# One token group of the shared expert moved behind the routed experts

## The chip, the cores and the metric

The kernel runs on one core of a Trainium2 chip. The core has a matrix engine (TensorE, PE in the profile), a vector engine (VectorE, DVE), an activation engine (ScalarE, ACT), a general one (GpSimd, POOL) and a synchronising one that here only issues transfers (SyncE, SP). Each runs its own stream of instructions in order and waits for the others on semaphores. Weights, tokens and results lie in device memory (HBM); work is done in on-chip memory (SBUF) and in the accumulators of TensorE (PSUM). The metric is the device time of the kernel in microseconds.

## The reference

Inputs are `x`, 32 sequences of 100 tokens of 512 values, and a context of which the causal mask leaves the first 100 positions. A layer norm, a cross-attention of 16 heads with an output product `Wfc` and a residual come first. Then, with `hs` the layer norm of that sum:

```
logits = hs @ gate_w.T                      # 16 experts
scores = softmax(logits)                    # per token
topk_w, topk_idx = top_k(scores per sequence and expert, 12)
g, u   = x_tok @ Wg[e].T, x_tok @ Wu[e].T   # the 12 tokens of each sequence, hidden size 1024
eo     = ((gelu(g) * u) @ Wd[e].T) * topk_w
out    = scatter_add(eo)                    # to the tokens they came from
shared = (gelu(hs @ Ws_g.T) * (hs @ Ws_u.T)) @ Ws_d.T
result = x + out + shared
```

Each of the 16 experts so works on 32 x 12 = 384 tokens, three tiles of 128. The shared expert works on all 3200 tokens, 25 tiles.

## The kernel before, in words

All products are in float32, made of three products of split operands (a high part and the remainder): `mm3`, line 55. So every weight and every activation is split once, by a cast on ScalarE and a subtraction on VectorE.

The attention stage (to about 430 us) writes its result to device memory, tensor `yD`. The feed-forward stage is the class `FeedForward`, method `run`. Its order is written out by hand for TensorE, ScalarE, VectorE and SyncE; GpSimd's order is chosen by the scheduler. The stage is a row of jobs: first nine jobs for the shared expert, one for each group of tiles in `GROUPS` (3, 2, 2, 3, 3, 3, 3, 3, 3 tiles), then 16 jobs for the routed experts, each of three tiles.

A job (`job`) has eight steps, one for each 128 hidden values. A step does the gate and up products (`gate_up`, 24 products into the PSUM tiles "gu"), then what is listed for this step under `mid`, then the down products of the step before (`down`, into "dn", 3 products for each tile), then what is listed under `post`. Gelu, multiplication and split (`hidden`: tiles g, hh, hl) run on ScalarE and VectorE while TensorE does the next products. After the last step's down products each tile goes to a sink. A job's last down products stand in step 0 of the next job.

- `shared_sink` adds the product to the residual on VectorE (line 759) and stores the sum to `out` by SyncE (line 760).
- `expert_sink` scales on ScalarE (line 792) and adds into `out` by an indirect transfer that GpSimd issues (line 793).

The lists `mid` and `post` hold the work that goes on beside the products:

- Preparation of the next group (class `Prep`): load y (step 0), load x, add the bias on GpSimd, split y (step 1), the output product `fc` (steps 2 to 4), layer norm `ln` one tile per step, store of the normed token to `xnD`, transposition and split `turn` two steps after `fc`, then `logits` and `tokens` in step 7. `tokens` puts the logits of the group into the table `LG`.
- Routing (class `Route`), in the last group's job: the softmax over `LG` after the job before it, the transposes of the scores (`turn`, line 938, copies of line 940, stores to `sD`) in steps 0 and 1, the load of the scores by sequence (`load`), the top-8 search twice (`top`) and an exchange through `rD` in step 2, the slot lists `isl` and `wsl` (`slots`) in step 4, the gather of expert 0's tokens by GpSimd (line 768), and their transposes (`gturn`, line 779) in step 7.
- In an expert's job: the gather and the transposes of the next expert's tokens.
- Weights: a chunk is the part of gate, up and down weights for one step, 768 KB. `chunk_load` asks for it (line 615, two raw buffers), `chunk_split` splits it (lines 626 and 627) into one of eight buffers `whl`, one per step. The shared expert's eight chunks are split once and stay for all nine groups. From the last group's job on, each step splits the chunk of the next job.

The small PSUM tiles "m" of `fc`, the transposes and the logits share two buffers. The tiles "big" (y, the scores, gathered tokens) share two, the split tokens xh and xl share two, the tiles x1 six.

Of the kernel before, what the change touches and what calls it, by code (L numbers as in the profile page):

```python
# [7 lines left out]
F32 = mybir.dt.float32  # L8
# [3 lines left out]
ALU = mybir.AluOpType  # L12
# [27 lines left out]
def f32(ap):  # L40
    return ap.bitcast(F32)
# [495 lines left out]
class FeedForward:  # L537
# [4 lines left out]
    def __init__(self, tc, K, top):  # L542
        self.tc, self.K, self.nc = tc, K, tc.nc
        self.starts = [sum(GROUPS[:g]) for g in range(len(GROUPS))]
        self.sw, self.raws, self.asked, self.nxt = {}, {}, 0, 0
        self.pend = None
# [12 lines left out]
        self.LG = wfp.tile([128, T // 128, NE], F32, name="LG")  # L559
        self.stacks = [top.enter_context(ExitStack()) for _ in range(3)]  # L560
# [49 lines left out]

    def chunk_load(self):
        n = self.asked
        if n < NFC * (self.K.ne + 1):
            self.raws[n] = self.rawp.tile([128, 3 * D], F32, name="wraw")
            self.nc.sync.dma_start(self.raws[n], self.K.wE[n // NFC, n % NFC])
            self.asked += 1

    def chunk_split(self, n, part=None):
# [79 lines left out]

    def run(self):
        self.open_rest()  # L700
        ng = len(GROUPS)
        for g, nt in enumerate(GROUPS):
            mid, post = {}, {}

            def at(d, f, *calls):
                d.setdefault(f, []).extend(calls)

            if g == 0:
                for f in range(NFC - 2):
                    at(post, f, lambda f=f: self.chunk_split(f + 2))  # L710
            if g + 1 < ng:
                p = self.prep(g + 1)
                at(post, 0, p.load_y, *[lambda i=i: p.load_x(i) for i in range(p.nt)])
                at(post, 1, *[lambda i=i: p.bias(i) for i in range(p.nt)])
                at(post, 1, p.split_y)
                for i in range(p.nt):
                    at(mid, 2 + i, lambda p=p, i=i: p.fc(i))
                    at(post, 2 + i, lambda p=p, i=i: p.ln(i))
                    at(post, 3 + i, lambda p=p, i=i: p.store(i))
                    at(mid, 4 + i, lambda p=p, i=i: p.turn(i))  # L720
                at(mid, 7, p.logits)
                at(post, 7, p.tokens)
            if g == ng - 1:
                r = Route(self)
# [11 lines left out]
            self.job(0, xh, xl, nt, self.shared_sink(self.starts[g], x1s), mid, post)  # L736
            if g + 1 < ng:
                self.ready[g + 1] = p.done()
            if g + 2 == ng:
                Route.softmax(self)  # L740
        self.route = r
        for e in range(self.K.ne):
            mid, post = {}, {}
            if e + 1 < self.K.ne:
                at(post, 0, lambda: self.gather(e + 1, r))
                for i in range(NST):
                    at(mid, 3 + i, lambda i=i: self.gturn(e + 1, i))
                at(post, 0, lambda: self.chunk_split(NFC * (e + 2) - 1))
                for f in range(1, NFC):
                    at(post, f, lambda f=f: self.chunk_split(NFC * (e + 2) + f - 1))  # L750
            else:
                at(post, 0, lambda: self.chunk_split(NFC * (e + 2) - 1))
# [52 lines left out]
class Prep:  # L805
# [30 lines left out]
    def bias(self, i, eng=None):  # L836
        (eng or self.F.nc.gpsimd).tensor_tensor(self.xb[i], self.xb[i], self.F.bfc, ALU.add)  # L837
# [38 lines left out]
    def store(self, i):  # L876
        self.F.nc.sync.dma_start(self.F.K.xn[self.rows(i), :], self.xn[i])

    def turn(self, i):
        F, nc, cs = self.F, self.F.nc, slice(i * 128, (i + 1) * 128)  # L880
        if self.xh is None:
            self.xh, self.xl = F.xt_tiles()
        tv = self.pt()
        for d in range(NC4):
            nc.tensor.transpose(tv[:, d, :], self.xn[i][:, d * 128:(d + 1) * 128], F.K.ident)
        nc.scalar.copy(self.xh[:, :, cs], tv)
        nc.vector.tensor_tensor(self.xl[:, :, cs], tv, f32(self.xh[:, :, cs]), ALU.subtract)
# [23 lines left out]
        return self.xh, self.xl, [self.xb[i] for i in range(self.nt)]  # L911


class Route:


    def __init__(self, F):
        self.F, self.nc = F, F.nc

    @staticmethod  # L920
    def softmax(F):
# [9 lines left out]
    def turn(self, b0, nb):  # L931
        F, nc = self.F, self.nc
        so = F.bigp.tile([128, NC4, GMAX], F32, name="big").rearrange("p c t -> p (c t)")
        for t0 in range(0, nb, 4):
            nt = min(4, nb - t0)
            tb = F.ps_m.tile([128, D], F32, name="m")
            for i in range(nt):
                nc.tensor.transpose(tb[0:NE, i * 128:(i + 1) * 128], F.LG[:, b0 + t0 + i, :],
                                    F.K.ident)
            nc.vector.tensor_copy(so[0:NE, t0 * 128:(t0 + nt) * 128], tb[0:NE, 0:nt * 128])  # L940
        nc.sync.dma_start(F.K.sD[:, b0 * 128:(b0 + nb) * 128], so[0:NE, 0:nb * 128])

    def load(self):
        F, nc = self.F, self.nc
# [38 lines left out]
@with_exitstack  # L983
def tile_kernel(ctx, tc, x, ctxT, wA, wE, bfc, gwT, ident, mask, base, out):
    nc = tc.nc
    K = Env()
    K.nsb, K.ne = NSB, NE
    K.x, K.ctxT, K.wA, K.wE, K.bfc, K.gwT, K.mask, K.base, K.out = \
        x, ctxT, wA, wE, bfc, gwT, mask, base, out
    dram = ctx.enter_context(tc.tile_pool(name="dram", bufs=1, space=bass.MemoryType.DRAM))  # L990
    K.kD = dram.tile([128, NC4, T], F32, name="kD")
    K.vD = dram.tile([T, D], F32, name="vD")
    K.yD = dram.tile([NC4, 128, T], F32, name="yD")
    K.xn = dram.tile([T, D], F32, name="xnD")
    K.sD = dram.tile([NE, T], F32, name="sD")
# [56 lines left out]
```

## Time and profile before

| | |
|---|---|
| Median of three runs | 1749.06 us (1748.99 to 1749.1) |
| The profiled execution | 1750.64 us |
| Its span, first to last instruction | 1748.8 us |
| Granted clock of TensorE | 0.987 |
| TensorE busy | 1698.7 us, 97% |
| VectorE, ScalarE, GpSimd busy | 885.7, 681.2, 445.0 us |
| Moved by all transfers | 211.13 MB, 121 GB/s on average |
| Idle of TensorE from 846.4 to 911.1 us (last group's job, routing) | 64.70 - 59.97 = 4.73 us |
| Idle of TensorE from 489.6 to 536.8 us (a two-tile group) | 47.20 - 46.17 = 1.03 us |

How to read the lines shown below. A line of the timeline has the start, the duration, engine and source line, operation, "output <- inputs" by the program's names, shapes, a count and, in brackets, how long the engine was idle before it and who ended that. A line of the waits has the waiting engine and line, who was waited for, the total in us, the number of waits and the longest. "PE" is the product, "PEld" its weight load, "SPq" or "POOLq" the instruction queue of an engine. Line 1048 is the end of the program: each engine drains, and the engines exchange semaphores. A line of that list has the count, the shortest, middle and longest duration in ns, and the start of the first and of the last.

### The profile page before, as it was taken

What the parts mean: (1) busy time and instruction counts of PE and PEld (TensorE: products, weight loads), DVE (VectorE), ACT (ScalarE), POOL (GpSimd) and SP (SyncE); (2) the same over time, 40 slices, a digit from 0 to 9 for tenths busy, and PEclk for the clock granted to TensorE, in tenths of its full rate; (3) what the DMA queues carried; (4) which work ended last, traced back from release to release, by engine and by line L of the source; (5) the groups of instructions that cost most, each with busy time, mean ns of one, the idle gap of its engine ahead of it and who ended that gap; (6) DMA issues with size and microseconds to landing.
All of it is one profiled execution on the core that took longest, in us unless ns stands there. A gap on an engine that the chain in (4) does not pass through costs nothing.

```text
span 1748.8 us, 27994 instructions
## 1 busy us (share of the span) xinstructions
PE 1698.7 (97%) x11072; PEld 1559.6 (89%) x11072; DVE 885.7 (51%) x2118; ACT 681.2 (39%) x1086; POOL 445.0 (25%) x399
## 2 busy tenths in 40 slices
PE   7999999989999999999999999999999999999996
PEld 6888888878888999999889999999999999999996
DVE  4877777775333333333454444444444444444431
ACT  4555555543112111211234444444444444444431
POOL 3777777661111011101020111110111111011111
PEclk9999999989999999999999999999999999999998
DMA  7444443534111101102154555554555554555531
GB/s 211 136 137 155 131 131 118 164 109 134 70 63 59 55 31 67 61 19 73 46 185 142 163 141 153 158 158 148 148 159 147 163 153 143 156 162 137 137 88 18
DMA packets 82995, 211.13 MB, mean 121 GB/s; under 512 B 9489, under 2 KB 35842, under 8 KB 82864
## 3 DMA queue, kind: packets, MB, share of 16 engines
q1 hardware_dynamic: 71792, 183.87, 32.2%
q0 software_dynamic: 10784, 25.21, 7.9%
q8 instruction: 87, 1.43, 0.3%
q14 instruction: 44, 0.36, 0.1%
q10 hardware_dynamic: 288, 0.27, 0.0%
HBM read 163.71 MB, written 45.60 MB: 120 GB/s over the span
## 4 chain that ended last, share of the span: by engine, by line
PE 91%; DVE 3%; DMA 2%; POOL 2%; ACT 1%; issue 1%; SPq 0%; POOLq 0%; ACTq 0%; DVEq 0%
PE gu L55 46%; PE dn L55 23%; PE kv L55 10%; PE m L55 3%; PE ms L277 2%; PE sc L236 2%; PE ms L292 1%; POOL p L256 1%; DMA big<-yD 1%; PE m L779 1%; DVE p L247 1%; PE ms L167 1%; DVE xt L161 1%; DMA kD<-kk 1%; PE m L894 1%
## 5 line engine op out<-in xcount | busy, mean ns | idle before, releaser
L55 PE MATMUL gu<-xh,whl 128*128 128x384 f32 (+1 forms) x3200 | 645.0, 333 | 1.3 <-ACT g L654 1.3
L55 PEld LDWEIGHTS gu<-xh,whl 128*128 128x128 f32 x3200 | 559.0, 188 | 18.8 <-ACT g L654 1.5
L55 PE MATMUL dn<-whl,hh 128*128 128x512 f32 x1168 | 372.4, 400 | 0.0
L627 DVE TENSOR_TENSOR whl<-wraw,whl 128x1536 fp32r<-128x1536 f32 (+1 forms) x138 | 242.1, 1755 | 241.9 <-ACT whl L626 241.8
L55 PE MATMUL gu<-xl,whl 128*128 128x384 f32 (+1 forms) x1600 | 338.1, 333 | 0.0
L55 PEld LDWEIGHTS gu<-xl,whl 128*128 128x128 f32 x1600 | 280.8, 188 | 0.0
L655 DVE TENSOR_TENSOR g<-g,gu 128x384 f32<-128x384 f32 (+1 forms) x200 | 108.7, 544 | 319.1 <-PE gu L55 316.8
L658 ACT CAST hh<-g 128x384 fp32r<-128x384 f32 (+1 forms) x200 | 100.9, 505 | 431.8 <-DVE g L655 431.8
L55 PEld LDWEIGHTS dn<-whl,hh 128*128 128x128 f32 x1168 | 213.3, 189 | 37.3
L626 ACT CAST whl<-wraw 128x1536 fp32r<-128x1536 f32 (+1 forms) x138 | 201.4, 1460 | 105.3 <-PE dn L55 103.4
L55 PE MATMUL dn<-whl,hl 128*128 128x512 f32 x584 | 230.9, 395 | 0.0
L654 ACT ACTIVATE g<-gu 128x384 f32<-128x384 f32 (+1 forms) x200 | 96.7, 484 | 312.5 <-PE gu L55 312.4
L793 POOL DMA_INDIRECT out_dram<-x,isl x48 | 77.5, 1615 | 365.5 <-ACT x L792 355.8
L659 DVE TENSOR_TENSOR hl<-g,hh 128x384 fp32r<-128x384 f32 (+1 forms) x200 | 111.8, 559 | 114.2 <-ACT hh L658 114.2
L768 POOL DMA_INDIRECT big<-xnD,isl x48 | 48.7, 1015 | 422.5 <-PE m L779 351.8
L55 PEld LDWEIGHTS dn<-whl,hl 128*128 128x128 f32 x584 | 109.8, 188 | 25.9
L271 POOL TENSOR_TENSOR p<-p,sm 100x800 f32<-100x800 f32 x64 | 101.2, 1583 | 51.0 <-DVE sm L266 36.6
L256 POOL TENSOR_TENSOR p<-p,mx 100x800 f32<-100x800 f32 x64 | 96.5, 1528 | 49.7 <-DVE mx L247 49.7
L837 POOL TENSOR_TENSOR x<-x,bfc 128x512 f32<-128x512 f32 x24 | 44.4, 1875 | 248.4 <-DMA x<-x 248.4
L247 DVE CUSTOM_DVE_ANT_0 p<-sc,mask 100x100 f32<-100x100 f32 x512 | 95.6, 257 | 16.6 <-PE sc L236 16.6
L265 DVE TENSOR_REDUCE sm<-p 100x8 f32<-100x800 f32 x64 | 62.7, 980 | 14.1 <-ACT p L260 14.1
L260 ACT ACTIVATE p<-p 100x800 f32<-100x800 f32 x64 | 56.2, 879 | 17.3 <-POOL p L256 17.3
(138 smaller groups left out, 1650.7 us busy)
## 6 DMA issues: line engine op xcount, KB each, us to landing
wraw<-wE SPq DMA_DIRECT2D x136, 768.0 KB, 4.5
xt<-x SPq DMA_DIRECT2D x32, 200.0 KB
vD<-vt SPq DMA_DIRECT2D x25, 256.0 KB, 2.1
kt<-kD SPq DMA_DIRECT2D x32, 200.0 KB, 4.9
v<-vD SPq DMA_DIRECT2D x8, 800.0 KB
x<-x SPq DMA_DIRECT2D x25, 256.0 KB, 5.1
xnD<-xn SPq DMA_DIRECT2D x25, 256.0 KB, 2.0
out_dram<-x SPq DMA_DIRECT2D x25, 256.0 KB, 2.2
```

The lines of the kernel that those rows point to most:

```text
L55: r = nc.tensor.matmul(out, t[0][a], t[1][b], start=(first and i == 0), stop=(last and i == n - 1))
L247: nc.vector.tensor_tensor_reduce(out=p[:, bb, h, :], in0=sc[:, h, cs], in1=mask, scale=ISCALE, scalar=NEG, op0=ALU.add, op1=ALU.max, accum ...
L256: nc.gpsimd.tensor_tensor(pv, pv, mx[:, :, None].to_broadcast([S, 8, S]), ALU.subtract)
L265: nc.vector.tensor_reduce(sm, pv, AX.X, ALU.add)
L271: nc.gpsimd.tensor_tensor(pv, pv, sm[:, :, None].to_broadcast([S, 8, S]), ALU.mult)
L626: nc.scalar.copy(h[:, cs], r[:, cs])
L627: nc.vector.tensor_tensor(l[:, cs], r[:, cs], f32(h[:, cs]), ALU.subtract)
L654: nc.scalar.activation(g[:, 0:t], pg[:, 0:t], AF.Gelu)
L655: nc.vector.tensor_tensor(g[:, 0:t], g[:, 0:t], pu[:, 0:t], ALU.mult)
L658: nc.scalar.copy(hh[:, 0:t], g[:, 0:t])
L659: nc.vector.tensor_tensor(hl[:, 0:t], g[:, 0:t], f32(hh[:, 0:t]), ALU.subtract)
L793: ins = nc.gpsimd.indirect_dma_start(out=self.K.out, out_offset=bass.IndirectOffsetOnAxis(ap=r.isl[:, i:i + 1], axis=0), in_=o, in_offset= ...
```

## The change

The groups become 3, 2, 3, 3, 3, 3, 3, 3, 2 tiles. Eight of them are worked on as before; the last, of two tiles, is the late group.

- Class `Late` extends `Prep`. Its y, its x (into a "big" tile) and its bias are asked for in steps 5 and 6 of group 5's job; the split of y stands in step 7. In group 6's job stand `fc` (steps 0 and 1), `ln`, the stores of the normed tokens and of the residual to `out`, `turn` (steps 2 and 3), the store of xh and xl to a new tensor `xT` (step 3), `logits` and `tokens` (step 4).
- The preparation of group 7 stands in the same job, one step later than usual; its `logits` and `tokens` move into step 0 of group 7's job, with the softmax behind them.
- Routing stands in group 7's job. `Route.turn` now takes eight, eight, eight and one blocks, partly under `mid` and partly under `post`, in steps 1 and 2. The load, the search, the slots and the gather come one step later than before; the first transposes of gathered tokens stay in step 7.
- The shared expert's chunks are loaded a second time, as a 17th expert's would be: seven are split in the steps of expert 15's job, one in the late group's step 0.
- A last job does the late group's products. xh and xl come back from `xT` (asked for in step 0 of expert 15's job). Its sink adds the product to what stands in `out` (asked for in step 5, after all scatters) and stores the sum.

The core of the diff:

```diff
-GROUPS = [3, 2, 2, 3, 3, 3, 3, 3, 3]
+GROUPS = [3, 2, 3, 3, 3, 3, 3, 3, 2]
...
-        if n < NFC * (self.K.ne + 1):
+        if n < NFC * (self.K.ne + 2):
+            e = n // NFC % (self.K.ne + 1)
...
+                if g + 2 == ng:
+                    z = 1
+                    q = self.late
+                    for i in range(q.nt):
+                        at(mid, i, lambda i=i: q.fc(i))
+                        at(post, i, lambda i=i: q.ln(i))
+                        at(post, 1 + i, lambda i=i: q.store(i))
+                        at(mid, 2 + i, lambda i=i: q.turn(i))
+                    at(post, 3, q.keep)
+                    at(mid, 4, q.logits)
+                    at(post, 4, q.tokens)
...
+            if g + 3 == ng:
+                q = self.late = Late(self, ng)
+                at(post, 5, q.load_y)
+                at(post, 6, q.bias)
+                at(post, 7, q.split_y)
...
-                at(mid, 0, lambda: r.turn(0, 12))
-                at(mid, 1, lambda: r.turn(12, 12), lambda: r.turn(24, 1))
-                at(post, 1, r.load)
-                at(post, 2, *[lambda j=j: r.top(j) for j in range(4)], r.exchange)
-                at(mid, 4, r.slots)
-                at(post, 4, lambda: self.gather(0, r))
+                at(mid, 0, p.logits)
+                at(post, 0, p.tokens, lambda: Route.softmax(self))
+                at(mid, 1, lambda: r.turn(0, 8))
+                at(post, 1, lambda: r.turn(8, 4, True), lambda: r.turn(12, 4))
+                at(mid, 2, lambda: r.turn(16, 8, True))
+                at(post, 2, lambda: r.turn(24, 1, True), r.load)
+                at(post, 3, *[lambda j=j: r.top(j) for j in range(4)], r.exchange)
+                at(mid, 5, r.slots)
+                at(post, 5, lambda: self.gather(0, r))
...
             else:
-                at(post, 0, lambda: self.chunk_split(NFC * (e + 2) - 1))
+                at(post, 0, self.late.load)
+            at(post, 0, lambda: self.chunk_split(NFC * (e + 2) - 1))
+            for f in range(1, NFC):
+                at(post, f, lambda f=f: self.chunk_split(NFC * (e + 2) + f - 1))
...
+        q, ne = self.late, self.K.ne
+        xh, xl = self.xg
+        self.job(ne + 1, xh, xl, q.nt, q.sink, {},
+                 {0: [lambda: self.chunk_split(NFC * (ne + 2) - 1)], 5: [q.load_out]})
         self.down()
...
+class Late(Prep):
...
+    def store(self, i):
+        super().store(i)
+        self.F.nc.sync.dma_start(self.F.K.out[self.rows(i), :], self.xb[i])
...
+    def keep(self):
+        n = self.nt * 128
+        for k, t in enumerate((self.xh, self.xl)):
+            self.F.nc.sync.dma_start(self.F.K.xT[k], f32(t[:, :, 0:n]))
...
+    def load_out(self):
+        F = self.F
+        self.o = []
+        for i in range(self.nt):
+            o = F.x1p.tile([128, D], F32, name="x1")
+            F.nc.sync.dma_start(o, F.K.out[self.rows(i), :])
+            self.o.append(o)
+
+    def sink(self, i, ps):
+        F = self.F
+        F.nc.vector.tensor_tensor(self.o[i], ps, self.o[i], ALU.add)
+        F.nc.sync.dma_start(F.K.out[self.rows(i), :], self.o[i])
```

More of the change, by code (lines that the diff above doesn't have):

```diff
@@ L545, in __init__ @@
         self.sw, self.raws, self.asked, self.nxt = {}, {}, 0, 0
-        self.pend = None
+        self.pend = self.late = None
         self.scat = {}
@@ L612, in chunk_load @@
         n = self.asked
-        if n < NFC * (self.K.ne + 1):
+        if n < NFC * (self.K.ne + 2):
             self.raws[n] = self.rawp.tile([128, 3 * D], F32, name="wraw")
-            self.nc.sync.dma_start(self.raws[n], self.K.wE[n // NFC, n % NFC])
+            e = n // NFC % (self.K.ne + 1)
+            self.nc.sync.dma_start(self.raws[n], self.K.wE[e, n % NFC])
             self.asked += 1
@@ L700, in run, with at @@
         self.open_rest()
-        ng = len(GROUPS)
-        for g, nt in enumerate(GROUPS):
+        ng = len(GROUPS) - 1
+        def at(d, f, *calls):
+            d.setdefault(f, []).extend(calls)
+        for g in range(ng):
             mid, post = {}, {}
-            def at(d, f, *calls):
-                d.setdefault(f, []).extend(calls)
             if g == 0:
@@ L712, in run @@
                 p = self.prep(g + 1)
-                at(post, 0, p.load_y, *[lambda i=i: p.load_x(i) for i in range(p.nt)])
-                at(post, 1, *[lambda i=i: p.bias(i) for i in range(p.nt)])
-                at(post, 1, p.split_y)
-                for i in range(p.nt):
[L717 to L720, printed above, removed]
@@ L721, in run @@
-                at(mid, 7, p.logits)
-                at(post, 7, p.tokens)
-            if g == ng - 1:
-                r = Route(self)
-                at(mid, 0, lambda: r.turn(0, 12))
-                at(mid, 1, lambda: r.turn(12, 12), lambda: r.turn(24, 1))
-                at(post, 1, r.load)
-                at(post, 2, *[lambda j=j: r.top(j) for j in range(4)], r.exchange)
-                at(mid, 4, r.slots)
-                at(post, 4, lambda: self.gather(0, r))
+                z = 0
@@ new lines, in run @@
+                at(post, z, p.load_y, *[lambda i=i: p.load_x(i) for i in range(p.nt)])
+                at(post, z + 1, *[lambda i=i: p.bias(i) for i in range(p.nt)])
+                at(post, z + 1, p.split_y)
+                for i in range(p.nt):
+                    f = z + 2 + i
+                    at(mid, f, lambda p=p, i=i: p.fc(i))
+                    at(post, f, lambda p=p, i=i: p.ln(i))
+                    at(post, min(f + 1, 7), lambda p=p, i=i: p.store(i))
+                    at(mid, min(f + 2, 7), lambda p=p, i=i: p.turn(i))
@@ new lines, in run @@
+                if z == 0:
+                    at(mid, 7, p.logits)
+                    at(post, 7, p.tokens)
+            if g + 3 == ng:
[3 more added lines that the diff above has]
+                at(post, 7, q.split_y)
+            if g == ng - 1:
+                r = self.route = Route(self)
+                at(mid, 0, p.logits)
[7 more added lines that the diff above has]
+                at(post, 5, lambda: self.gather(0, r))
@@ L735, in run @@
             xh, xl, x1s = self.ready.pop(g)
-            self.job(0, xh, xl, nt, self.shared_sink(self.starts[g], x1s), mid, post)
+            self.job(0, xh, xl, GROUPS[g], self.shared_sink(self.starts[g], x1s), mid, post)
             if g + 1 < ng:
                 self.ready[g + 1] = p.done()
-            if g + 2 == ng:
-                Route.softmax(self)
-        self.route = r
         for e in range(self.K.ne):
@@ L747, in run @@
                     at(mid, 3 + i, lambda i=i: self.gturn(e + 1, i))
-                at(post, 0, lambda: self.chunk_split(NFC * (e + 2) - 1))
-                for f in range(1, NFC):
-                    at(post, f, lambda f=f: self.chunk_split(NFC * (e + 2) + f - 1))
-            else:
-                at(post, 0, lambda: self.chunk_split(NFC * (e + 2) - 1))
+            else:
+                at(post, 0, self.late.load)
+            at(post, 0, lambda: self.chunk_split(NFC * (e + 2) - 1))
+            for f in range(1, NFC):
+                at(post, f, lambda f=f: self.chunk_split(NFC * (e + 2) + f - 1))
             xh, xl = self.xg
             self.job(e + 1, xh, xl, NST, self.expert_sink(e), mid, post)
+        q, ne = self.late, self.K.ne
+        xh, xl = self.xg
+        self.job(ne + 1, xh, xl, q.nt, q.sink, {},
+                 {0: [lambda: self.chunk_split(NFC * (ne + 2) - 1)], 5: [q.load_out]})
         self.down()
@@ L911, in done, with __init__, load_y, bias @@
         return self.xh, self.xl, [self.xb[i] for i in range(self.nt)]
+class Late(Prep):
+    def __init__(self, F, g):
+        m = lambda: F.ps_m.tile([128, D], F32, name="m")
+        super().__init__(F, g, m, lambda: m().rearrange("p (c t) -> p c t", c=NC4))
+    def load_y(self):
+        F = self.F
+        super().load_y()
+        x = F.bigp.tile([128, NC4, GMAX], F32, name="big").rearrange("p c t -> p (c t)")
+        for i in range(self.nt):
+            self.xb[i] = x[:, i * D:(i + 1) * D]
+            F.nc.sync.dma_start(self.xb[i], F.K.x[self.rows(i), :])
+    def bias(self):
+        for i in range(self.nt):
+            super().bias(i)
+    def store(self, i):
+        super().store(i)
+        self.F.nc.sync.dma_start(self.F.K.out[self.rows(i), :], self.xb[i])
+    def turn(self, i):
+        if i == 0:
+            self.xh, self.xl = self.F.xt_tiles()
+            self.F.nxt -= 1
+        super().turn(i)
+    def keep(self):
+        n = self.nt * 128
+        for k, t in enumerate((self.xh, self.xl)):
+            self.F.nc.sync.dma_start(self.F.K.xT[k], f32(t[:, :, 0:n]))
+    def load(self):
+        F, n = self.F, self.nt * 128
+        F.xg = F.xt_tiles()
+        for k, t in enumerate(F.xg):
+            F.nc.sync.dma_start(f32(t[:, :, 0:n]), F.K.xT[k])
+    def load_out(self):
+        F = self.F
+        self.o = []
+        for i in range(self.nt):
+            o = F.x1p.tile([128, D], F32, name="x1")
+            F.nc.sync.dma_start(o, F.K.out[self.rows(i), :])
+            self.o.append(o)
+    def sink(self, i, ps):
+        F = self.F
+        F.nc.vector.tensor_tensor(self.o[i], ps, self.o[i], ALU.add)
+        F.nc.sync.dma_start(F.K.out[self.rows(i), :], self.o[i])
 class Route:
@@ L918, in __init__ @@
         self.F, self.nc = F, F.nc
+        self.so = None
     @staticmethod
@@ L929, in softmax, with turn @@
         nc.vector.tensor_tensor(LG, LG, sm[:, 1, :, None].to_broadcast([128, NT, NE]), ALU.mult)
-    def turn(self, b0, nb):
+    def turn(self, b0, nb, store=False):
         F, nc = self.F, self.nc
-        so = F.bigp.tile([128, NC4, GMAX], F32, name="big").rearrange("p c t -> p (c t)")
-        for t0 in range(0, nb, 4):
-            nt = min(4, nb - t0)
+        if self.so is None:
+            self.so = F.bigp.tile([128, NC4, GMAX], F32, name="big").rearrange("p c t -> p (c t)")
+            self.at = b0
+        for t0 in range(b0, b0 + nb, 4):
+            nt = min(4, b0 + nb - t0)
+            o = (t0 - self.at) * 128
             tb = F.ps_m.tile([128, D], F32, name="m")
             for i in range(nt):
[L938 to L941, printed above, removed]
+                nc.tensor.transpose(tb[0:NE, i * 128:(i + 1) * 128], F.LG[:, t0 + i, :], F.K.ident)
+            nc.vector.tensor_copy(self.so[0:NE, o:o + nt * 128], tb[0:NE, 0:nt * 128])
+        if store:
+            n = b0 + nb - self.at
+            nc.sync.dma_start(F.K.sD[:, self.at * 128:(self.at + n) * 128],
+                              self.so[0:NE, 0:n * 128])
+            self.so = None
     def load(self):
@@ L994, in tile_kernel @@
     K.xn = dram.tile([T, D], F32, name="xnD")
+    K.xT = dram.tile([2, 128, NC4, GROUPS[-1] * 128], F32, name="xTD")
     K.sD = dram.tile([NE, T], F32, name="sD")
```

## The prediction

> **What bounds the kernel now.** I read the page first (engine shares, the chain that ended last), then the waits of PE, then two stretches of the timeline: the routing group and the last microseconds.
>
> ```profile
> span 1748.8 us, 27994 instructions
> PE 1698.7 (97%) x11072; PEld 1559.6 (89%) x11072; DVE 885.7 (51%) x2118; ACT 681.2 (39%) x1086; POOL 445.0 (25%) x399
> PE 91%; DVE 3%; DMA 2%; POOL 2%; ACT 1%; issue 1%; SPq 0%; POOLq 0%; ACTq 0%; DVEq 0%
> ```
>
> TensorE is busy 97% of the span and carries 91% of the chain. A change that leaves its work alone can gain only where TensorE stands still. After the attention stage (from 430 us) there are few such places. The waits of PE from 838 to 960 us, the routing group and the first expert:
>
> ```profile
> PE m L938 <- DVE big L940: 3.1, 2, 1.6
> PE m L779 <- DVE xl L784: 1.6, 1, 1.6
> ```
>
> The 3.1 us are the transposes of the routing scores (`Route.turn`). Twelve stand in a row, there are only two PSUM buffers "m", and the copies that empty them stand on DVE behind the hidden products:
>
> ```profile
> 850.72 1.03 PE L938 MATMUL m<-ident,LG 128*16 128x128 f32 x8
> 852.12 0.56 DVE L659 TENSOR_TENSOR hl<-g,hh 128x384 fp32r<-128x384 f32 x1 [0.58 <-ACT hh L658]
> 852.60 2.05 DVE L940 COPY big<-m 16x512 f32<-16x512 f32 x3
> 853.33 0.60 PE L938 MATMUL m<-ident,LG 128*16 128x128 f32 x4 [1.57 <-DVE big L940]
> ```
>
> The largest idle stretch is the end. The last product, the three scatters that follow it, and the closing instructions of the program (line 1048):
>
> ```profile
> 1734.75 0.40 PE L55 MATMUL dn<-whl,hl 128*128 128x512 f32 x1
> 1734.74 1.55 POOL L793 DMA_INDIRECT out_dram<-x,isl  x1 [40.57 <-ACT x L792]
> 1736.60 1.55 POOL L793 DMA_INDIRECT out_dram<-x,isl  x1 [0.30 <-issue]
> 1738.46 1.55 POOL L793 DMA_INDIRECT out_dram<-x,isl  x1 [0.30 <-issue]
> ...
> L1048 SPq EVENT_SEMAPHORE  x3: 27/28/1827, 1742.2 to 1744.1; - x3
> ...
> L1048 POOLq DRAIN  x3: 46/97/12125, 1735.9 to 1748.6; - x3
> ```
>
> TensorE ends at 1734.75 + 0.40 = 1735.15; the span ends at 1748.8. That is 13.65 us of tail. SP sees the last scatter landed at about 1744.1 (its wait that began at 1742.2 lasted 1.83). GpSimd's drain, begun at 1735.9, lasts 12.125 us, to 1748.06. The closing exchange of semaphores among the engines then takes 0.75 us.
>
> **The change, part by part.**
>
> *TensorE's work: 0.* Before, the groups are seven of three tiles and two of two; so they are after, in another order. Products, transposes and logits are as many. A two-tile step costs the same at the end as in the middle: 451.62 to 455.85 = 4.23 us, of which gate and up 2.85, down 1.38.
>
> *The tail: -9.35 us.* The last thing computed is now a shared group. Its sink is one DVE addition and one plain store on SP, in place of an ACT copy and an indirect accumulate on GpSimd. After the last product: 0.05 to the addition (the ACT copy started 0.03 behind its product), 0.70 addition (three sinks of line 759 take 2.10), 0.06 to SP, 2.4 from issue to landing (the stores of 855.38; the median of all is 2.2), 0.3 for SP to see it and drain, 0.75 closing exchange: 4.3 us against 13.65. The three scatters of expert 15 move to step 0 of the late group. From the first sink (1733.78) to the landing they take 10.3 us, to the end of the drain 14.3. The late group runs 2.85 + 2.10 (expert 15's last down) + 7 x 4.23 + 1.38 = 35.9 us, so both are covered. Without that cover they would cost what they cost now.
>
> Here a rule speaks against the row. The Trainium skill, "VectorE: DVE Perf Modes", section "The DRAIN you can't avoid", says that drains of the program's pre- and postamble take a constant 12 ns or so on every engine. If so, GpSimd's drain hides nothing of its own and the 4.0 us between SP's landing (1744.1) and 1748.06 are a fixed closing cost that stays: the tail becomes 8.3 and the gain 5.35. The row says otherwise: the other engines' drains here are 7 to 20 ns, or end with their engine's last instruction, and GpSimd alone shows 12,125 ns, begun as its scatters were issued. I take the row, -9.35, and keep -5.35 as the other end.
>
> *Routing: -3.1 + 0.5.* `Route.turn` now puts at most eight transposes in a row (two buffers) and the rest behind the next down products. The 3.1 go. But logits, tokens and softmax now stand in step 0 of the group that also adds the previous group's three sinks on DVE. Count from the end of that step's gate/up products: logits 1.4, down 2.1, tokens 0.3, next gate/up 4.27, so TensorE wants the scores at 8.07. DVE: lt addition done at 2.64 (as at 842.58 to 845.22 now), three sinks 2.10, token copy 0.21, then softmax (token copy's start to last multiply 3.55 now): 4.75 + 3.55 = 8.3. A stall of 0.25, and up to 0.25 more for the buffers of the second batch: I take 0.5, between 0 and 1.5. The 1.6 at line 779 stays, because three gather transposes still stand together in step 7. The top-8 search, the exchange and the slots all move one step later together, so their distances stay. Only the gather comes one step (6.35 us) nearer to its transposes. Its issues were at 886.40, 887.83 and 889.52 and land 4.3 us later (the third at 893.8); the transposes ran at 901.83 to 904.47. Of about 11 us of slack, 4.5 remain: cost 0.
>
> *Preparation of the late group in groups 5 and 6: 0.* Every instruction counts: 24 fc products, 8 transposes, 8 logits products and 2 token transposes on PE (moved, not added); on DVE and ACT two fc additions, statistics, normalisations, splits; on SP one yD load, two x loads, two xn stores, and new: two stores of out (256 KB each), two of xT (512 KB each). The heaviest step of group 6 gives DVE a 2.27 us y split, 0.69 transposed split and 1.11 hidden work, 4.1 us in a step of 6.9. The late y split stands behind a token copy, done 4.2 us after gate/up of group 5's step 7 (842.58 to 846.77 for the last group now); with 1.93 for yl it is ready at 6.1, and fc wants it at 1.4 + 2.1 + 0.3 + 4.25 = 8.05. The group's inputs x are in a "big" tile, released by the out stores long before routing takes it. Behind the xT stores on SP stand only later xn stores and loads. The bound is -0 to +3: if each of five fc's waited as the worst one now does (0.85 us at 502 us), 4 us; nearest to 0, since three-tile groups show no such wait.
>
> *Group 2 has three tiles: -0.3.* Only one two-tile group now hosts a preparation. Before, two did: fc began 0.3 late in group 1 (459.02) and 1.0 + 0.35 late in group 2 (502.26, 504.57). Group 1 now hosts a three-tile preparation, so it takes over 1.35; the 0.3 goes.
>
> *Second load of the shared weights: 0.* Eight loads of 768 KB, eight casts on ACT (1.46) and subtractions on DVE (1.76). Seven splits fall into expert 15's steps, which have none now; the other experts carry the same load with TensorE fully busy (100.00 of 100 us, DVE 48, ACT 44). One falls into late step 0, seven steps ahead of its use. Uncovered they would cost about 8 x 1.8 = 14 us on DVE.
>
> *Late loads: 0.* xT (two of 512 KB) is asked for at step 0 of expert 15. Its tile was last read by expert 14, so there is no long wait; seven weight loads queue behind it on SP. These have slack: SP waits 777 us over 132 loads, 5.9 us each, for a buffer, and two transfers of 512 KB cost once about what one of 768 KB does, 4.4 us. The load of out (step 5) waits for the scatters; behind it are the two final stores. It is asked for 4.95 + 5 x 4.23 = 26 us into the late group; the scatters have landed at about 3.7 + 10.3 = 14; with the 5.1 us of an x load it is there at 31, and its first use is at 35. The cover is 4 us; without it each us late costs one.
>
> **Sum** against the profiled execution: 1748.8 - 9.35 - 3.1 + 0.5 - 0.3 = 1736.55 span. The profiled run took 1750.64 in all, 1.84 more than its span; the median of the runs without a profile is 1749.06. I subtract the 12.25 us from that: **1736.8 us** (-0.70%).
>
> **Rivals.**
>
> *The closing cost is fixed* (the drain rule holds): 1736.8 + 4.0 = 1740.8. For it: in this trace the drain always follows scatters, so one can't see what it does alone. Against it: only GpSimd has it.
>
> *The crowded group 6 or routing stalls.* PE stands still at fc or at line 938 by up to 4 + 1 us: 1739 to 1742. For it: two "m" buffers and engines in order, as the 3.1 us show. Against it: every reuse of a buffer is a step apart.
>
> *The transfers are the loss: nothing gained.* The out load comes later than 35 us into the late group, or the last weights do, and the tail's gain goes into waiting: 1746 to 1749.
>
> *Slower: the expert path starts late.* Place: the gather transposes of expert 0 in step 7 of the routing group. Routing starts in the group's step 0 as before, but each part stands a step later while step 7 stays. Four transfers through memory (sD out, sD in, rD out, rD in) and the gather are in series. Price: 1 us per us beyond the 4.5 us of slack, since all TensorE work waits behind it. It decides from 4.5 + 12.25 = 17 us of delay, three steps of 6.35: 1736.8 + 19 - 4.5 = 1751. For it: the gather's landing has a maximum of 9.1 us and weight loads share the queues. Against it: 9.1 instead of 4.3 just uses the slack.
>
> **How the numbers follow.** Likeliest 0.66 (1734.5 to 1739); fixed closing 0.14; stalls 0.10; nothing gained 0.04; slower 0.06. The range reaches through the fixed closing and most of the stalls: 1734.5 to 1742. About 0.2% (3.5 us) can be told from no change here; faster by that means below 1745.5. Faster 0.90 (the first three), same 0.04, slower 0.06.
>
> **What would show it.** In the profile after: GpSimd's last scatter some 36 us before the end and no drain of microseconds in the last stretch; last product to end of span 4 to 5 us; line 1020 (the turn) without the 3.1 us; at most 0.5 us of wait before its first transposes; the two-tile late group at about 4.25 us per step without a wait for whl or xh. I would be wrong if GpSimd's closing still ends 4 us behind the landing, if fc waits in group 6, or if the out load lands behind the last product.

## The result and the profile after

The changed kernel takes 1736.74 us (median of 4 runs, 1733.68 to 1736.99) against 1749.08 us before: a ratio of 0.9925, 95% interval 0.9913 to 0.9937. The forecast was 1736.8. Two later series on one chip each with the kernel before gave 1734.98 against 1750.4 (0.9913, interval 0.9899 to 0.9926) and 1734.15 against 1751.06 (0.9909, 0.9896 to 0.9923). So the gain is between 12 and 17 us; the forecast's 12.25 lies at the lower edge of that. The section on the stages shows which part of these numbers is scatter.

The page of the profiled execution, the same three lines as before (it took 1736.99 us in all):

```profile
span 1735.2 us, 28064 instructions
PE 1698.0 (98%) x11072; PEld 1559.9 (90%) x11072; DVE 900.6 (52%) x2126; ACT 692.2 (40%) x1094; POOL 442.3 (25%) x399
PE 93%; DVE 2%; POOL 2%; DMA 1%; ACT 1%; issue 1%; SPq 0%; ACTq 0%; POOLq 0%; DVEq 0%
```

TensorE has the same 11072 products and the same busy time within a microsecond. VectorE and ScalarE have 15 and 11 us more, about what the eight splits of the second weight load take (14.0 and 11.8 us more on their two lines). What went is idle time. After the attention stage two waits of PE are left, and the turn of the scores is not among them:

```profile
PE m L803 <- DVE xl L808: 1.6, 1, 1.6
PE m L55 <- ACT yh L850: 0.9, 1, 0.9
```

The timeline of the routing group, with the first token copy, the end of the softmax and the transposes:

```profile
819.60 0.18 DVE L931 COPY LG<-m 128x48 f32<-128x48 f32 x1
...
822.56 0.57 DVE L1008 TENSOR_TENSOR LG<-LG,rsm 128x400 f32<-128x400 f32 x1
...
823.46 1.03 PE L1020 MATMUL m<-ident,LG 128*16 128x128 f32 x8
...
825.34 1.27 DVE L1021 COPY big<-m 16x512 f32<-16x512 f32 x2
...
826.43 1.04 PE L1020 MATMUL m<-ident,LG 128*16 128x128 f32 x8
```

The softmax ends at 823.13 and TensorE arrives at 823.46, so nothing stalls here. The second batch starts at 826.43 behind the down products. The first of its two buffers had been emptied by then (826.01), the second was at 826.61, before its turn came.

The end of the timeline, and three lines of the closing instructions (line 1134 now):

```profile
1730.81 1.39 DVE L988 TENSOR_TENSOR x<-dn,x 128x512 f32<-128x512 f32 x2 [0.71 <-PE dn L55]
1731.07 0.40 PE L55 MATMUL dn<-whl,hl 128*128 128x512 f32 x1
1731.53 1.03 SPq L989 DMA_DIRECT2D out_dram<-x  x2
...
L1134 POOLq DRAIN  x3: 46/97/12680, 1701.1 to 1734.9; - x3
L1134 SPq DRAIN  x3: 7/7/7, 1734.4 to 1734.7; - x3
```

TensorE ends at 1731.47, the span at 1735.2: a tail of 3.73 us against 13.65. GpSimd's long drain is still there, 12.68 us, but it runs from 1701.1 to 1713.8, beside the late group's products.

### The profile page after: what moved, and what is told of

It reads as the page before. It is cut to its first block, busy times and chain, and to the rows that moved or that the text cites. A ratio compares the mean times of both kernels' runs of the same rounds, so it can differ in the third digit from the quotient of the medians.

```text
span 1735.2 us, 28064 instructions
## 1 busy us (share of the span) xinstructions
PE 1698.0 (98%) x11072; PEld 1559.9 (90%) x11072; DVE 900.6 (52%) x2126; ACT 692.2 (40%) x1094; POOL 442.3 (25%) x399
## 4 chain that ended last, share of the span: by engine, by line
PE 93%; DVE 2%; POOL 2%; DMA 1%; ACT 1%; issue 1%; SPq 0%; ACTq 0%; POOLq 0%; DVEq 0%
PE gu L55 47%; PE dn L55 23%; PE kv L55 10%; PE m L55 4%; PE ms L277 2%; PE sc L236 2%; PE ms L292 2%; POOL p L256 1%; PE m L803 1%; DVE p L247 1%; DVE xt L161 1%; PE ms L167 1%; DMA kD<-kk 1%; PE m L918 1%; PE m L909 1%
## 5 line engine op out<-in xcount | busy, mean ns | idle before, releaser
L628 DVE TENSOR_TENSOR whl<-wraw,whl 128x1536 fp32r<-128x1536 f32 (+1 forms) x146 | 256.1, 1754 | 253.5 <-ACT whl L627 253.4
L627 ACT CAST whl<-wraw 128x1536 fp32r<-128x1536 f32 (+1 forms) x146 | 213.2, 1460 | 109.9 <-PE dn L55 108.9
L861 POOL TENSOR_TENSOR x<-x,bfc 128x512 f32<-128x512 f32 x22 | 38.7, 1786 | 185.0 <-DMA x<-x 185.0
```

The lines of the kernel that those rows point to most:

```text
L627: nc.scalar.copy(h[:, cs], r[:, cs])
L628: nc.vector.tensor_tensor(l[:, cs], r[:, cs], f32(h[:, cs]), ALU.subtract)
```

## Where the time went, by stage

Three marks can be found in every profile: the first gate product, the first token transposes in the feed-forward stage, and the end of the last product. (The text above lets the attention stage last to about 430 us. In the kernel before, its last product starts at 393.5, beside the first gate products.) Microseconds, each from one profiled execution:

| kernel | first gate product | first token transposes | from there to the last product's end | tail |
|---|---|---|---|---|
| before | 383.86 | 446.34 | 1288.81 | 13.65 |
| changed | 385.24 | 447.73 | 1283.74 | 3.73 |
| changed, second run | 385.01 | 447.79 | 1283.67 | 3.74 |
| changed, third run | 384.66 | 447.30 | 1283.83 | 3.77 |
| turn alone | 382.54 | 443.88 | 1284.83 | 13.69 |
| plain end alone | 387.06 | 450.03 | 1289.16 | 4.01 |
| GpSimd stores | 384.48 | 447.20 | 1283.79 | 8.31 |
| no second load | 383.40 | 445.95 | 1283.83 | 3.72 |
| out load paced | 383.51 | 446.13 | 1283.81 | 5.76 |
| gather later | 382.09 | 444.90 | 1288.39 | 3.71 |
| two waits less | 384.02 | 447.13 | 1280.40 | 4.27 |
| two waits less, again | 383.43 | 444.12 | 1280.39 | 4.29 |

All these kernels run the same work up to the first token transposes (the version of the last two rows asks for one more transfer ahead of them), yet these stand anywhere between 443.88 and 450.03. This is scatter, and it makes the whole times differ by some microseconds. The granted clock goes with it: from the first gate product to the token transposes it was 1.00 in the two executions that were quick there (turn alone 61.3 us, the last row 60.7), and 0.97 in the ten others (62.5 to 63.1). From 300 us to the first gate product it was 0.90 in the latest one (387.06) and 0.93 and 0.94 in the two earliest. Behind the mark it is 1.00 before and after the change, and the three executions of the changed kernel repeat the stretch within 0.2 us. The change is worth 5.07 us of stretch and 9.92 us of tail, 15.0 in all; in the pair of profiles first compared, 1.4 of them were hidden by a later mark. TensorE's idle time in the stretch is 6.07 us before, 2.52 after and nothing in the last two rows. Its busy time there, of the same 6915 products, fell by 1.5 as well: part of a standstill is counted in the durations of products, and so the next section also looks at the weight loads.

## The experiments

Expectations speak of the prediction's terms. "Theory" in them is: TensorE's idle stretches are the whole of the gain, and everything added is hidden.

**The turn alone.** The kernel before, with the new `Route.turn` in its old place.

```diff
-                at(mid, 0, lambda: r.turn(0, 12))
-                at(mid, 1, lambda: r.turn(12, 12), lambda: r.turn(24, 1))
-                at(post, 1, r.load)
+                at(mid, 0, lambda: r.turn(0, 8))
+                at(post, 0, lambda: r.turn(8, 4, True), lambda: r.turn(12, 4))
+                at(mid, 1, lambda: r.turn(16, 8, True))
+                at(post, 1, lambda: r.turn(24, 1, True), r.load)
```

> The kernel before with one part of the change alone: the score transposes in batches of at most eight, some behind the down products, in the same group and steps 0 and 1. My theory: the queue of the weight loads shows 4.0 us of wait at these transposes (the products only 3.1), and these 4.0 us go one for one: ratio 0.9977, span 1744.8, no wait left at the turn. The prediction's own term said 3.1, 1745.7. Rival: the wait only moves to the search or the gather behind it: no change, 1748.8.

Measured: 1745.98 us, ratio 0.9973 (0.9965 to 0.9982); the stretch fell by 3.98 us, the tail stayed. The number that fits is not the wait of the products but that of the weight loads, which the waits of the queue "PEld" show. Before:

```profile
PEld m L938 <- DVE big L940: 4.0, 3, 1.9
PEld m L905 <- issue: 2.6, 7, 0.4
PEld m L55 <- ACT yh L826: 1.8, 3, 1.1
PEld m L779 <- DVE xl L784: 1.8, 1, 1.8
PEld m L55 <- DVE yl L827: 1.4, 3, 0.6
PEld m L905 <- DVE so L898: 0.4, 1, 0.4
```

In the kernel with the turn alone the first line is gone, and the sum of the others has changed by 0.1. In the changed kernel it is gone, too, and the others have become:

```profile
PEld m L929 <- issue: 2.2, 6, 0.4
PEld m L803 <- DVE xl L808: 1.8, 1, 1.8
PEld m L55 <- ACT yh L850: 1.1, 1, 1.1
PEld m L55 <- DVE yl L851: 0.7, 2, 0.4
PEld m L929 <- DVE so L922: 0.4, 1, 0.4
PEld m L929 <- DVE x L783: 0.4, 1, 0.4
```

4.0 for the turn and 3.2 - 1.8 = 1.4 for fc make 5.4, where the stretch fell by 5.07. The line with `DVE x` is no new wait: the token transposes (L905, now L929) have eight waits of 0.4 in both kernels, and one of them is now put down to the sinks' additions. The rival (the wait moves on to the search or the gather) falls. What the turn is worth is shown by this run. The order of the groups was not run alone: what is left for it is 5.07 - 3.98 = 1.09. Its waits at fc follow the order in every profile, though: 3.1 to 3.6 us in the three kernels with the old order, 1.6 to 1.9 in those with the new one (the last version, which takes them away, left aside).

**A plain end alone.** The kernel before; expert 15's results are stored plainly by SyncE to rows 0 to 383 of `out`.

```diff
             nc.scalar.activation(o, ps, AF.Copy, scale=r.wsl[:, i:i + 1])
+            if e == self.K.ne - 1:
+                nc.sync.dma_start(self.K.out[j * 128:(j + 1) * 128, :], o)
+                return
```

> The kernel before, with expert 15's three results written by plain stores from SyncE to rows 0 to 383 of out, in place of the indirect accumulates from GpSimd (part of the computation is so replaced). No group is moved. My theory: the tail of 13.65 us is the scatters' issue, their landing and GpSimd's drain; with plain stores the last product is followed by a ScalarE copy of 0.7, a store of 2.1 and a closing of 1 us: tail 4 us, span 1739.1, ratio 0.9945. Rival (fixed closing cost): tail 8, span 1743.1.

Measured: 1740.0 us, ratio 0.9938 (0.9923 to 0.9954), tail 4.01 us, stretch as before (+0.35; its waits at fc are 3.6 instead of 3.2). GpSimd's long drain, 12.44 us from 1693.7, ends at 1706.1 beside expert 15's products. The profiled span, 1743.2, is longer than expected because its attention stage was the longest of all (387.06); behind the marks the expectation holds. The tail's gain needs no moved group, only that the last thing isn't a scatter. The moved group is what makes that possible with the right result.

**The last stores by GpSimd.** The changed kernel; only the queue of the two last stores differs.

```diff
-        F.nc.sync.dma_start(F.K.out[self.rows(i), :], self.o[i])
+        F.nc.gpsimd.dma_start(F.K.out[self.rows(i), :], self.o[i])
```

> The changed kernel, its two last stores issued by GpSimd instead of SyncE, as plain stores. Theory A (GpSimd's drain follows any transfer that GpSimd has issued): tail 3.7 + 1 to 2 of issue + about 4 of drain behind the landing, 9 us, span 1740 to 1741. Theory B (only the indirect accumulates bring it): tail 5 us, span 1736.5.

Measured: 1740.78 us, ratio 0.994 (0.9925 to 0.9955), tail 8.31 us. The stores in the timeline, and the closing lines:

```profile
1731.32 1.29 POOL L989 DMA_DIRECT2D out_dram<-x  x2 [26.20 <-DVE x L988]
...
L1134 POOLq DRAIN  x3: 46/103/6532, 1732.0 to 1739.0; - x3
L1134 SPq DRAIN  x3: 7/7/7, 1734.7 to 1738.8; - x3
```

SyncE has seen everything landed at 1734.7; GpSimd's drain goes on to 1732.0 + 6.53 = 1738.5, 3.8 us longer. Theory A holds: the drain follows plain stores too, and it reaches some 4 us behind the landing, as it did in the kernel before (1744.1 to 1748.06). The changed kernel has a third case: its last scatter has landed at 1709.7, and the drain ends at 1713.8. Of the tail's 9.9 us these are 4; the remaining 5.9 are the scatters' own issue and landing. A fixed closing cost on every engine, the prediction's first rival, falls with the changed kernel's own tail and with the plain end: neither has it.

**No second load.** The changed kernel; the late group uses expert 15's weights, still on the chip (so its result is another), and eight loads and splits are left out.

```diff
-        if n < NFC * (self.K.ne + 2):
+        if n < NFC * (self.K.ne + 1):
...
-            for f in range(1, NFC):
+            for f in range(1, NFC if e + 1 < self.K.ne else 1):
                 at(post, f, lambda f=f: self.chunk_split(NFC * (e + 2) + f - 1))
...
-        self.job(ne + 1, xh, xl, q.nt, q.sink, {},
-                 {0: [lambda: self.chunk_split(NFC * (ne + 2) - 1)], 5: [q.load_out]})
+        self.job(ne, xh, xl, q.nt, q.sink, {}, {5: [q.load_out]})
```

> The changed kernel without the second load of the shared weights: the late group uses expert 15's weights instead (its result so differs). Eight loads and splits fewer. My theory: they were hidden, so no change beyond 0.5 us: span 1735, ratio to the kernel before 0.993. Rival (they delay expert 15 or the late group): 2 us or more gained.

Measured: 1733.9 us (1732.0 to 1738.03), ratio 0.9906 (0.989 to 0.9922). The intervals with and without the load overlap, and the stretch decides: 1283.83 against 1283.67 to 1283.83. The 6.3 MB and the 26 us of splits cost nothing.

**The load of out, paced.** The changed kernel; the two loads go to ScalarE's queue, behind its work of step 7.

```diff
-                 {0: [lambda: self.chunk_split(NFC * (ne + 2) - 1)], 5: [q.load_out]})
+                 {0: [lambda: self.chunk_split(NFC * (ne + 2) - 1)], 7: [q.load_out]})
...
-            F.nc.sync.dma_start(o, F.K.out[self.rows(i), :])
+            F.nc.scalar.dma_start(o, F.K.out[self.rows(i), :])
```

> The changed kernel, with the two loads of the late group's rows of out issued by ScalarE behind its work of the last step, so paced by the products; on SyncE they were issued at 1709.75, as soon as the scatters had landed, 21 us before their use, though they were written in step 5. Theory: asked for at about 1729.7, there 3.4 us later, at 1733.1, against the first addition at 1730.8: 2.3 to 2.8 us lost, span 1737.5 to 1738. Rival (other work hides it still): 1735.2.

Measured: 1736.76 us, ratio 0.992 (0.9905 to 0.9935), tail 5.76 us, so 2.03 more. In the changed kernel's timeline the loads are issued in the late group's fourth step:

```profile
1709.75 0.81 SPq L983 DMA_DIRECT2D x<-out_dram  x2
```

In the paced kernel, loads and first addition:

```profile
1727.93 0.82 ACTq L983 DMA_DIRECT2D x<-out_dram  x2
...
1730.65 1.33 DVE L988 TENSOR_TENSOR x<-dn,x 128x512 f32<-128x512 f32 x2 [2.09 <-DMA x<-out_dram]
```

The last line names the transfer. Not all of its 2.09 us is loss: in the changed kernel VectorE stands still for 0.71 here as well, behind the product. So the first addition is 1.4 us late, and the end with it. The other 0.6 or so stands behind the additions: from the last store's issue to SyncE's drain it took 2.7 us (1732.1 to 1734.8), in the changed kernel 2.2; why is open. On SyncE there are 21 us between the load's issue and its use.

**The gather a step later.** The changed kernel with one step less of slack for expert 0's tokens.

```diff
-                at(mid, 5, r.slots)
-                at(post, 5, lambda: self.gather(0, r))
+                at(mid, 6, r.slots)
+                at(post, 6, lambda: self.gather(0, r))
```

> The changed kernel, with the slot lists and the gather of expert 0 one step (6.35 us) later again; its transposes stay in step 7. The prediction's working says 4.5 us of slack are left, in the profile of the changed kernel it is about 5: so 1.2 to 2 us are lost, span 1736.5 to 1737, and the wait before the gather transposes names the transfer. Rival (far more slack, or less because the gather meets the weight loads): no loss, or 5 us and more.

Measured: 1739.59 us, ratio 0.9938 (0.9923 to 0.9954); the stretch is 4.6 us longer than in the changed kernel, more than twice what I expected and close to the rival's 5. The gather's issues, the transposes, and the down products behind them:

```profile
857.28 1.13 POOL L792 DMA_INDIRECT big<-xnD,isl  x1 [61.78 <-DVE isl L1065]
...
859.98 1.65 POOL L792 DMA_INDIRECT big<-xnD,isl  x1 [0.30 <-issue]
...
862.44 0.63 PE L803 MATMUL m<-ident,big 128*128 128x128 f32 x4 [0.31 <-DMA big<-xnD,isl]
...
867.23 0.63 PE L803 MATMUL m<-ident,big 128*128 128x128 f32 x4 [4.16 <-DMA big<-xnD,isl]
867.61 1.06 PE L55 MATMUL dn<-whl,hh 128*128 128x512 f32 x2
```

The third transfer landed 7.2 us after its issue (859.98 to 867.2), not 4.3. Between 863.07 and 867.20, 92% of the transfer engines' time was taken, with the next expert's gather and a weight load on the way. That this made it late is not shown: in the changed kernel 89% was taken while the third transfer was on its way (858.41 to 862.81), and it landed in 4.4. The cost is read in the queue of the weight loads again:

```profile
PEld m L803 <- issue: 4.9, 2, 4.4
```

In the changed kernel these loads wait 1.8 us for VectorE, so the wait is 3.1 us longer. The rest, 1.5 us, starts in the last line of the timeline above and is told at the end: the products after the wait ran at about half speed.

**Two waits less.** The changed kernel; one gather transpose goes to the end of step 6, and group 2's y is asked for in group 0's job and split at the start of group 1's.

```diff
-                for i in range(NST):
-                    at(mid, 7, lambda i=i: self.gturn(0, i))
+                at(post, 6, lambda: self.gturn(0, 0))
+                at(mid, 7, lambda: self.gturn(0, 1), lambda: self.gturn(0, 2))
...
+                if g == 0:
+                    early = self.prep(2)
+                    at(post, 5, early.load_y)
+                if g == 1:
+                    p = early
+                    at(post, 0, p.split_y)
+                    at(post, 0, *[lambda i=i: p.load_x(i) for i in range(p.nt)])
+                    at(post, 1, *[lambda i=i: p.bias(i) for i in range(p.nt)])
...
```

> The changed kernel with two further waits taken away: the first gather transposes of expert 0 stand at the end of step 6, so that only two wait for two buffers in step 7 (1.8 us in the weight-load queue); and y of group 2 is asked for in group 0's job and split a step earlier, so that fc in the two-tile group doesn't wait for the split (1.1 + 0.4 us). Theory: 3.3 us less, span 1732, ratio to the kernel before 0.9906. Rival: the tokens of the gather aren't there at the end of step 6 and the first wait comes back there: only 1.5 us less.

Measured: 1732.11 us, ratio 0.9895 (0.9878 to 0.9912). Both waits are gone from the list, 2.5 us of the products or 3.6 of the weight loads; the transposes in the timeline:

```profile
857.94 0.60 PE L812 MATMUL m<-ident,big 128*128 128x128 f32 x4
...
862.57 1.04 PE L812 MATMUL m<-ident,big 128*128 128x128 f32 x8
```

The stretch is 1280.40, 3.3 us shorter. It was run again beside the changed kernel:

> The changed kernel without the two further waits, a second time, beside the changed kernel. In its first profile the stretch from the first token transposes to the last product took 1280.40 us against 1283.74 in the changed kernel. Theory: again 3.3 us less in that stretch, and a median some 3 us under the changed kernel's. Rival: the first difference was scatter of the attention stage and the end; nothing is left in the medians.

Measured: 1731.92 us (1730.55 to 1733.74), ratio 0.9895 (0.988 to 0.991), stretch 1280.39. The runs beside these two:

> The changed kernel again, beside the others on one chip. Theory: 1736.7 us, ratio 0.993. Its profile had 1.4 us more than the kernel before in the attention stage, where both run the same instructions; if that is scatter from run to run, it is gone or reversed here.

> The changed kernel a third time, for the comparison with the run beside it: 1735 to 1737 us, the stretch from the first token transposes to the last product 1283.7 us.

Measured 1734.98 and 1734.15 us. The later mark was neither gone nor reversed: the token transposes stand at 447.79 and 447.30, again 1.0 to 1.5 us behind the kernel before. The other versions of the changed kernel, with the same start, have them between 444.12 and 447.20, so this isn't put down to the change. The medians are 2.9 and 2.2 us apart in the two series, the intervals overlap a little, and the stretch repeats its 3.3 us. The tail is 0.5 us longer in both runs of this version (4.27 and 4.29). It stands behind the additions, between the last store's issue and SyncE's drain (2.6 us in both, 2.2 in the changed kernel); why is open. It is the fastest version here, and TensorE is busy for the whole of its stretch.

## Why the prediction was right

- *TensorE's work 0, second load 0, preparation of the late group 0.* Right. The run without the second load has the same stretch within 0.2 us. In groups 5 and 6 PE shows no wait at all, and its weight loads only the 0.4 at the token transposes that every group has.
- *Tail: -9.35.* Right in its mechanism, and -9.92 in size. The estimate of 4.3 us took 2.4 from issue to landing and 0.3 for SyncE; from the second issue (1732.22 by the additions' end at 1732.20) to SyncE's drain at 1734.4 it took 2.2 in all. That the row (12,125 ns) was taken against the rule on drains was right: with the rule the tail would have been 8.3, which only the version with GpSimd stores shows, and there for the drain's sake.
- *Routing: -3.1 + 0.5.* The mechanism was right, both sizes were off. The turn was worth 4.0: I read the waits of the products, but the wait of the weight load ahead of them is the longer one, and it is TensorE's real standstill. The stall of 0.25 at the first transposes didn't come, because the three sinks' additions began at 817.81, 2.40 after gate/up (815.41) instead of 2.64, and took 1.87 instead of 2.10, so that the token copy began at 4.19 instead of 4.75. The second quarter, for the buffers, was 0. The short wait of 0.4 behind the sinks' additions is not new, as the list above shows.
- *Group 2 has three tiles: -0.3.* The way was right, the size too small: -1.4 by the waits of the weight loads (3.2 before, 1.8 after), 1.1 by the stretches. Again the products' queue alone was read. It doesn't show a wait of 0.9 that the weight loads of the three-tile group behind had at fc (553 and 555 us), so that "three-tile groups show no such wait" was a misreading; after the change it is 0.4.
- *Late loads 0.* Right, by a wrong step. I had the load of out asked for 26 us into the late group, because it is written in step 5. SyncE isn't paced by the products: it ran ahead and asked at 1709.75, when the scatters had landed, 14.7 us after the group's first product. The cover was not 4 us but some 16 to 18, an estimate: the 21 us to its use, less the 2.7 us that it took in the paced kernel or the 5.1 of an x load.
- *Slack of the gather: 4.5.* Right: in the changed kernel the third transfer lands 4.4 us after its issue (858.41) and 4.1 us before its transposes (866.90). But the size rests on a landing that isn't steady. The run with the gather later shows 7.2 us, and such a landing would leave 1.3. The 9.1 us that the prediction names as the longest landing of a gather come from a list in which the scatters stand, too; the 48 gathers alone landed in 3.3 to 7.8 us. This was the place of the slower rival, and it is closer than the prediction made it.

The sum by stages is -15.0 where -12.25 was forecast; the three terms that were too small (tail by 0.6, routing by 1.4, group 2 by 0.8 to 1.1) account for the difference. That the first median fell on the forecast to 0.1 us was luck in part, by the scatter ahead of the feed-forward stage: later series, at 15.4 and 16.9 us of difference, agree better with the stages.

## What to carry to other kernels

When a kernel ends in transfers that one engine issues and then drains, put work that needs none of them between them and the end; the order of independent groups is free, and a group that ends in a plain store is the right last one. Read a standstill of TensorE in the queue of its weight loads, too, not only in that of its products. And compare stages between marks that both kernels share: here that resolved 0.2 us where whole times scattered by 3.

## What the runs showed of the hardware

GpSimd's drain ended about 4 us after the landing of the last transfer that it had issued, scatter or plain store: 3.96 us in the kernel before, 4.0 in the changed one, 3.8 with GpSimd stores (landings as SyncE saw them). From the end of the last issue it is no fixed time: 8.0, 8.1 and 5.9 us. The last drains of the other engines took nanoseconds (7 on SyncE). With the two last stores on GpSimd instead of SyncE, the tail was 8.31 us instead of 3.73.

A stand of 4.2 us slowed what came after it. Busy time by stretches for the kernel with the gather a step later (stretch and its length, busy time and count of PE, PEld, DVE, ACT and POOL, then the granted clock, the share and rate of transfers):

```profile
863.07:867.20 4.13, 0.00 (x0) 0.01 (x1) 1.63 (x3) 0.80 (x2) 2.08 (x2) 1.00 0.92 352
867.20:871.30 4.10, 4.07 (x13) 3.32 (x14) 0.69 (x1) 0.59 (x1) 2.56 (x3) 0.58 0.47 130
871.30:875.50 4.20, 4.20 (x25) 4.16 (x24) 1.76 (x1) 1.97 (x2) 0.28 (x1) 1.00 0.39 116
```

The clock granted to TensorE is 1.00 during the stand, 0.58 in the 4.1 us after it and 1.00 again after that; the nine down products took 3.7 us (867.61 to 871.34) instead of the 2.2 of the changed kernel (867.31 to 869.49). The stand of 1.6 us at the same place in the changed kernel left the clock at 1.00. This agrees with the Trainium skill, "TensorE: Matmul & The Clock Gate", section "What's actually happening", which gives half rate after an idle window of about 3.4 us. The long stand thus cost its own length and then about 1.5 us.
